# Attention inside a 1-core Trainium2 kernel: turned blocks of probabilities by 16 transfers a head between partitions, in place of five by way of memory

## The chip, the cores and the metric

One Trainium2 chip; the kernel uses one of its cores. A core has five engines that run side by side, each on its own instruction stream and in order: TensorE (PE, with the loading of its weights as PEld), VectorE (DVE), ScalarE (ACT), GpSimd (POOL) and SyncE (SP), which here does nothing but issue DMA transfers. The transfers themselves run on 16 DMA engines. Engines wait for one another and for transfers by semaphores.

The metric is the device time of one launch in microseconds (us), the median of the runs shown. Profiled executions are single executions with the hardware profiler on.

## The reference: what is computed

A transformer layer in float32, for 8 sequences of 512 tokens of width 256: attention with 16 query heads of width 128 in 4 groups (each group shares keys and values), then a feed-forward layer of 64 experts, six for a token, with a shared expert beside them. Each part has a normalization before and after it and a residual sum. Of the attention:

```python
q = q + pe
k = k + pe
scores = jnp.einsum('bgqtd,bgksd->bgqts', q, k) / math.sqrt(D)
causal = jnp.tril(jnp.ones((t, t), dtype=bool))
scores = jnp.where(causal, scores, -jnp.inf)
probs = jax.nn.softmax(scores, axis=-1)
out = jnp.einsum('bgqts,bgksd->btgqd', probs, v).reshape(b, t, G * QPG * D)
return out @ wo
```

The probabilities come out of the softmax with query tokens on the partitions. The product with `v` sums over key tokens, so it needs key tokens on the partitions: each 128 by 128 block of the probabilities has to be transposed. The change concerns how that is done.

## The kernel before

**Heads in a pipeline.** The outer loop (L884) runs over `k`, 0 to 127: 8 sequences of 16 heads. One iteration works on several heads at once, each at another step:

- `scores(k, i)` for the four tiles `i` of 128 query tokens (L887 and L888, then L893 and L894): TensorE multiplies queries and keys into `psc` (L280); DVE adds the causal mask, scales and finds the minimum into `e` (L284); ScalarE takes the exponential in place and sums rows (L287). Tile `i` has only its (i + 1) x 128 key columns, since the rest is masked.
- `turned(k - 1)` (L890), between the scores of tiles 1 and 2: the transposition, below.
- `weigh(k)` (L897): DVE takes reciprocals of the row sums (L294), GpSimd multiplies each `e` with them (L297).
- `project(k - 3)` (L900): the head's output times `wo`, summed over heads in PSUM (L352).
- `queries(k + 1)` (L907): the next head's queries, `pq` on TensorE (L267), bias and positions on DVE into `qt` (L270).
- `mix(k - 2)` (L909): probabilities times values into `pav` (L340), copied by ScalarE into `ao` (L108).

Between these, the loop calls the other work in small steps: the preparation of the next sequence (L929), the feed-forward part of the sequence before (`side`, L881), and, from head 94 on, the routed experts (`next(routed)`, L903 and others), 32 pairs of them, whose weights are loaded from memory by transfers that ScalarE issues (L515 and L522). After all pairs, the outputs of the first five sequences are finished with loads of `y_d` that SP issues (L650).

**Order.** The kernel is written with a schedule by hand: on each of the five engines, instructions run in the order in which the loop calls them. A DVE instruction that waits holds up every DVE instruction behind it, and a DMA that waits on SP holds up every DMA behind it on SP. Each transfer issued by SP or ScalarE counts up one of eight completion counters, given out in turn.

**Turning a head.** `e` holds 10 blocks of 128 by 128 on or under the diagonal. DVE's transpose turns squares of 32 by 32 in place, inside a group of 32 partitions. Six such instructions (L313) write the head into `eb`, laid out as (partition, `c`, block, `t`), where `c` says which group of 32 key tokens a square belongs to, and where the partition's group `a` says which group of 32 query tokens. A square is then right in itself, but stands in partition group `a`; for the product it has to be in group `c`. So squares must move from group to group, all 16 pairs (`c`, `a`), 32 partitions by 10 blocks x 32 values (1280 bytes) each. The kernel before does it through memory: SP stores `eb` whole into `ex_d` (L317, 640 KB; two such buffers), waits for it, and loads it back with four transfers (L320), one for each `c`, 32 partitions by four rows of 1280 bytes, into `et`. `mix` reads `et`.

`eb` has one buffer, `et` two, and each `e` two. The last two heads don't go this way: TensorE transposes them (`turned_at_once`, L323).

Of the kernel before, what the change touches and what calls it, by code (L numbers as in the profile page):

```python
# [22 lines left out]
NI = T // P  # L23
BS = 32
# [19 lines left out]
def sandwich_kernel(ctx, tc, x, wq, bq_t, wkv, bk_t, bv, wo, gate_wt, w_gate, w_up, w_down,  # L44
                    sh_gate_t, sh_up_t, sh_down_t, pe_t, out):
    nc = tc.nc
# [13 lines left out]
    ex_d = [dram.tile([P, NI, NB * BS], F32, tag=f"ex{n}_d", name=f"ex{n}_d") for n in range(2)]  # L60
# [61 lines left out]
    with ExitStack() as part:  # L122
# [180 lines left out]
        def turned(k):  # L303
            l = live[k]
            eb = p2.tile([P, NI, NB, BS], F32, tag="eb", name=f"eb_{k}", bufs=1)
            for i in range(NI):
                for js in ([0, 1], [2, 3]):
                    js = [j for j in js if j <= i]
                    if not js:
                        continue  # L310
                    at, step = AT[js[0]] + i - js[0], AT[js[-1]] - AT[js[0]] - 1
                    blocks = eb[:, :, at : at + step * (len(js) - 1) + 1 : max(step, 1), :]
                    nc.vector.transpose(  # L313
                        blocks.rearrange("p c j t -> p j c t"),
                        l["e"][i][:, js[0] * P : (js[-1] + 1) * P].rearrange("p (j c t) -> p j c t", c=NI, t=BS))
            ex = ex_d[k % 2]
            nc.sync.dma_start(out=ex, in_=eb.rearrange("p c n t -> p c (n t)"))  # L317
            l["et"] = p2.tile([P, NI, NB, BS], F32, tag="et", name=f"et_{k}")
            for c in range(NI):
                nc.sync.dma_start(out=l["et"][ts(c, BS)].rearrange("s a n t -> s a (n t)"),  # L320
                                  in_=ex[:, c, :].rearrange("(a s) f -> s a f", s=BS))

        def turned_at_once(k):  # L323

# [559 lines left out]
        for k in range(NK):  # L884
            b, s = divmod(k, NH)
# [3 lines left out]
            if 0 <= k - 1 < NK - 2:  # L889
                turned(k - 1)  # L890
# [136 lines left out]
```

## Time and profile before

| | us |
|---|---|
| median of 3 runs | 1485.7 |
| lowest and highest of them | 1483.86, 1485.82 |
| the profiled execution's own time | 1494.1 |
| its span, first to last instruction | 1492.3 |

Prediction and profile are compared by the profiled execution; it is 8.4 us above the median.

What the head loop's instructions take in it:

| Line | Engine | What | Count | Mean ns of one |
|---|---|---|---|---|
| L280 | PE | scores | 1024 | 445 |
| L340 | PE | probabilities times values | 1024 | 433 |
| L352 | PE | output projection | 1024 | 382 |
| L267 | PE | queries | 512 | 593 |
| L284 | DVE | mask, scale, minimum | 512 | 479 |
| L313 | DVE | transposes of 32 by 32 squares | 756 | 364 |
| L287 | ACT | exponential | 512 | 559 |
| L297 | POOL | weighing | 508 | 570 |

How to read the profile: the page has one line per engine (busy time, its share of the span, instructions), groups of instructions, and transfers by queue. The queue on which SP's transfers run moved 206.76 MB of 252.03 in all; memory was read for 143.01 MB and written for 107.74. In lists of waits, "A <- B: t, n, m" says that A waited t us in total for B, in n waits, the longest m us. In a timeline, "SPq" is SP's issuing of a transfer, not the transfer itself. Groups give the shortest, median and longest duration in ns.

### The profile page before, as it was taken

How to read it: one execution, taken by the hardware profiler on the slowest of the kernel's cores; microseconds unless marked ns; L12 is line 12 of the kernel's file. 1: busy time of each engine (PE TensorE's matmuls, PEld its weight loads, DVE VectorE, ACT ScalarE, POOL GpSimd, SP SyncE). 2: the span in 40 equal slices, each digit the busy share in tenths (PEclk: the TensorE clock that was granted, in tenths of full speed). 3: DMA queues.
4: the chain of work that ended last, by engine and by line, in shares of the span. 5: the costliest groups of instructions: out<-in, count | busy, mean ns of one | idle time of the engine just before them, and what ended most of it. 6: DMA issues, size and time to landing. Idle time of an engine off the chain costs nothing. (4 is left out here: it accounts for less than half of the span.)

```text
span 1492.3 us, 18593 instructions
## 1 busy us (share of the span) xinstructions
PE 1409.6 (94%) x5350; PEld 860.8 (58%) x5350; DVE 890.7 (60%) x3094; ACT 499.5 (33%) x1434; POOL 427.4 (29%) x682
## 2 busy tenths in 40 slices
PE   7999999999999999999999999988899998898894
PEld 3566655666656665666566666554555655565652
DVE  4565576657665676557665766665455454567442
ACT  1333343233332342233323332232333343344322
POOL 1222231124112322123112321144434344534202
PEclk9999999999999999999999999999999999999987
DMA  5764554355544464355435544469998899777511
GB/s 204 220 192 140 153 169 139 106 155 166 147 139 134 147 185 124 121 159 173 136 104 160 164 146 125 138 190 247 240 243 224 241 255 248 175 239 220 179 43 65
DMA packets 159702, 252.03 MB, mean 169 GB/s; under 512 B 16092, under 2 KB 135869, under 8 KB 159341
## 3 DMA queue, kind: packets, MB, share of 16 engines
q1 hardware_dynamic: 130061, 206.76, 46.5%
q10 hardware_dynamic: 23392, 34.61, 8.3%
q0 software_dynamic: 6144, 9.44, 3.4%
q8 instruction: 44, 0.72, 0.2%
q14 instruction: 61, 0.50, 0.1%
HBM read 143.01 MB, written 107.74 MB: 168 GB/s over the span
## 5 line engine op out<-in xcount | busy, mean ns | idle before, releaser
L297 POOL TENSOR_SCALAR e<-e,recip 128x128 f32<-128x128 f32 x508 | 269.6, 570 | 814.5 <-DVE recip L294 781.6
L287 ACT ACTIVATE e<-e,least 128x128 f32<-128x128 f32 (+3 forms) x512 | 285.8, 559 | 387.3 <-DVE least L284 356.0
L280 PE MATMUL psc<-kt,qt 128*128 128x128 f32 (+3 forms) x1024 | 312.7, 445 | 27.6 <-DVE least L284 8.7
L340 PE MATMUL pav<-et,v 128*128 128x512 f32 (+3 forms) x1024 | 297.2, 433 | 6.8 <-ACT dd L576 5.0
L340 PEld LDWEIGHTS pav<-et,v 128*128 128x128 f32 x1024 | 194.0, 190 | 170.1 <-issue 121.0
L284 DVE CUSTOM_DVE_ANT_0 e<-psc,mask 128x128 f32<-128x128 f32 (+3 forms) x512 | 231.7, 479 | 55.5 <-PE psc L280 49.6
L352 PE MATMUL po<-wo_sb,ao 128*128 128x256 f32 x1024 | 244.3, 382 | 0.7 <-ACT ao L108 0.7
L267 PE MATMUL pq<-xnt,wq_sb 128*128 128x512 f32 x512 | 240.8, 593 | 0.0
L352 PEld LDWEIGHTS po<-wo_sb,ao 128*128 128x128 f32 x1024 | 193.5, 191 | 69.3 <-issue 38.6
L280 PEld LDWEIGHTS psc<-kt,qt 128*128 128x128 f32 x1024 | 167.7, 193 | 108.7 <-DVE least L284 31.7
L313 DVE STREAM_TRANSPOSE eb<-e 128x128 f32<-128x128 f32 x756 | 227.4, 364 | 0.1
L108 ACT COPY ao<-pav 128x512 f32<-128x512 f32 x128 | 75.0, 586 | 445.3 <-PE pav L340 429.2
L270 DVE SCALAR_TENSOR_TENSOR qt<-pq,bq_sb,pe_sb 128x512 f32<-128x512 f32 x128 | 95.6, 747 | 115.0 <-PE pq L267 114.9
L267 PEld LDWEIGHTS pq<-xnt,wq_sb 128*128 128x128 f32 x512 | 95.9, 190 | 69.0 <-issue 63.5
L287 ACT ACTIVATION_READ_ACCUMULATOR e<-e,least 128x1 f32 x512 | 95.7, 187 | 0.0
L294 DVE RECIPROCAL recip<-total 128x4 f32<-128x4 f32 x128 | 22.8, 178 | 121.7 <-ACT e L287 121.7
L577 POOL DMA_INDIRECT y_d<-dd,idx x32 | 51.0, 1593 | 108.0 <-DMA y_d<-dd,idx 43.3
L239 PE MATMUL pk<-xnt,wkv_sb 128*128 128x512 f32 x128 | 61.3, 605 | 0.0
L252 DVE TENSOR_TENSOR v<-pv,bv_sb 128x512 f32<-128x512 f32 x32 | 22.1, 692 | 65.2 <-PE pv L250 65.2
L250 PE MATMUL pv<-wkv_sb,xnt 128*128 128x512 f32 x128 | 59.7, 593 | 0.0
L111 DVE COPY ht<-pth 88x256 f32<-88x256 f32 x32 | 13.4, 418 | 69.5 <-PE pth L558 69.4
L242 DVE SCALAR_TENSOR_TENSOR kt<-pk,bk_sb,pe_sb 128x512 f32<-128x512 f32 x32 | 24.0, 751 | 50.4 <-PE pk L239 50.4
(191 smaller groups left out, 1126.5 us busy)
## 6 DMA issues: line engine op xcount, KB each, us to landing
ex_d<-eb SPq DMA_DIRECT2D x126, 640.0 KB
et<-ex_d SPq DMA_DIRECT2D x504, 160.0 KB
wgu<-in_w_gate ACTq DMA_DIRECT2D x32, 352.0 KB
wgu<-in_w_up ACTq DMA_DIRECT2D x32, 352.0 KB
wd<-in_w_down ACTq DMA_DIRECT2D x32, 352.0 KB
y<-y_d SPq DMA_DIRECT2D x10, 512.0 KB
x<-in_x SPq DMA_DIRECT2D x8, 512.0 KB
x_d<-x SPq DMA_DIRECT2D x8, 512.0 KB
```

Of the source, the lines that this page charges most:

```text
L108: nc.scalar.copy(dst, src)
L239: nc.tensor.matmul(pk, lhsT=wkv_sb[:, c, g, 0, :], rhs=s["xnt"][:, c, :], start=c == 0, stop=c == NC - 1)
L250: nc.tensor.matmul(pv, lhsT=s["xnt"][:, c, ts(i, P)], rhs=wkv_sb[:, c, :, 1, :], start=c == 0, stop=c == NC - 1)
L267: nc.tensor.matmul(pq, lhsT=wq_sb[:, c, ts(h, D)], rhs=seqs[b]["xnt"][:, c, :], start=c == 0, stop=c == NC - 1)
L270: nc.vector.scalar_tensor_tensor(qt, pq, bq_sb[:, h : h + 1], pe_sb, ALU.add, ALU.add)
L280: nc.tensor.matmul(psc[:, :w], lhsT=l["qt"][:, ts(i, P)], rhs=seqs[b]["kt"][h // QPG][:, :w], start=True, stop=True)
L284: nc.vector.tensor_tensor_reduce(out=e, in0=psc[:, :w], in1=mask[:, T - w :], scale=-1.0 / math.sqrt(D), scalar=BIG, op0=ALU.add, op1=ALU. ...
L287: nc.scalar.activation(e, e, AF.Exp, bias=l["least"][:, i : i + 1], scale=-1.0, accum_out=l["total"][:, i : i + 1])
L297: engine.tensor_scalar(e, e, recip[:, n : n + 1], 1.0, ALU.mult, ALU.mult)
L313: nc.vector.transpose(blocks.rearrange("p c j t -> p j c t"), l["e"][i][:, js[0] * P : (js[-1] + 1) * P].rearrange("p (j c t) -> p j c t", ...
L340: nc.tensor.matmul(pav[:, :, j:, :], lhsT=seqs[b]["v"][:, j, ts(g, D)], rhs=l["et"][:, :, AT[j] : AT[j] + NI - j, :], start=j == 0, stop=j ...
L352: nc.tensor.matmul(po[b][i // 2][:, i % 2, :], lhsT=ao[:, ts(i, P)], rhs=wo_sb[:, h, :], start=h == 0 and i % 2 == 0, stop=h == NH - 1, sk ...
```

## The change

The store into `ex_d` and the four loads from it are gone. In their place SP issues 16 transfers for each head, one for every pair of groups, each from 32 partitions of `eb` straight into 32 partitions of `et`, 40 KB each. `ex_d` stays declared and unused. Nothing else is edited: the buffers, the six transposes and the readers of `et` are the same. In the built program the streams of PE, DVE, ACT and POOL hold the same instructions in the same order; only waits differ, since `eb` and `et` now each hang on 16 transfers.

```diff
@@ -313,12 +313,10 @@
                     nc.vector.transpose(
                         blocks.rearrange("p c j t -> p j c t"),
                         l["e"][i][:, js[0] * P : (js[-1] + 1) * P].rearrange("p (j c t) -> p j c t", c=NI, t=BS))
-            ex = ex_d[k % 2]
-            nc.sync.dma_start(out=ex, in_=eb.rearrange("p c n t -> p c (n t)"))
             l["et"] = p2.tile([P, NI, NB, BS], F32, tag="et", name=f"et_{k}")
             for c in range(NI):
-                nc.sync.dma_start(out=l["et"][ts(c, BS)].rearrange("s a n t -> s a (n t)"),
-                                  in_=ex[:, c, :].rearrange("(a s) f -> s a f", s=BS))
+                for a in range(NI):
+                    nc.sync.dma_start(out=l["et"][ts(c, BS), a], in_=eb[ts(a, BS), c])
 
         def turned_at_once(k):
 
```

## The prediction, made before the changed kernel ran

> **What bounds the kernel now.** The page comes first: who is busy.
>
> ```profile
> PE 1409.6 (94%) x5350; PEld 860.8 (58%) x5350; DVE 890.7 (60%) x3094; ACT 499.5 (33%) x1434; POOL 427.4 (29%) x682
> ```
>
> TensorE is busy 94% of the span. The table of busy time by stretch says where the other 6% lies; its columns are the stretch, its length, PE, PEld, DVE, ACT and POOL busy, the clock, the DMA share and GB/s.
>
> ```profile
> 37.00:174.00 137.00, 133.28 (x465) 82.10 (x465) 78.64 (x276) 48.66 (x144) 34.09 (x65) 1.00 0.60 177
> 496.00:657.00 161.00, 158.63 (x567) 98.24 (x566) 103.00 (x355) 54.07 (x161) 39.19 (x71) 1.00 0.48 145
> 980.00:1306.00 326.00, 302.38 (x1387) 175.53 (x1386) 175.98 (x631) 111.70 (x306) 142.89 (x166) 0.98 0.88 232
> ```
>
> A sequence of 16 heads (496 to 657) takes 161.0 us with 2.4 of TensorE idle: PE-bound, the path through memory hidden. In the expert stretch (980 to 1306) 23.6 us of TensorE are idle at a DMA share of 0.88. So no shorter path for the blocks can win much: up to 980 us there is almost nothing to win, after it at most some 25 us. The question is whether the new path stays hidden, so I read the queue that issues it, SP. Its waits:
>
> ```profile
> SPq L320 <- DMA ex_d<-eb: 443.0, 126, 9.3
> SPq L317 <- DVE eb L313: 436.2, 103, 9.8
> ```
>
> SP waits 443 us for the stores to memory (3.5 a head) and 436 us for the turned blocks: it has time to spare. Then its timeline over a sequence; columns are start, length, instruction, count. The reader is to see the distance from one store (L317) to the next.
>
> ```profile
> 495.86 0.34 SPq L317 DMA_DIRECT2D ex_d<-eb  x1
> 498.85 1.73 SPq L320 DMA_DIRECT2D et<-ex_d  x4
> 503.62 0.34 SPq L317 DMA_DIRECT2D ex_d<-eb  x1
> 511.38 0.34 SPq L317 DMA_DIRECT2D ex_d<-eb  x1
> ...
> 557.11 0.34 SPq L317 DMA_DIRECT2D ex_d<-eb  x1
> ...
> 570.24 0.34 SPq L317 DMA_DIRECT2D ex_d<-eb  x1
> ...
> 639.61 0.34 SPq L317 DMA_DIRECT2D ex_d<-eb  x1
> ...
> 649.09 0.34 SPq L317 DMA_DIRECT2D ex_d<-eb  x1
> ```
>
> A head takes 7.8 us where nothing else runs (503.62 to 511.38), 13.1 where a feed-forward step lies in it, 9.5 later on; the mean of 16 is 161/16 = 10.1. The whole timeline of one head shows what holds the one buffer `eb`:
>
> ```profile
> 705.48 1.81 DVE L313 STREAM_TRANSPOSE eb<-e 128x128 f32<-128x128 f32 x6
> ...
> 707.31 0.34 SPq L317 DMA_DIRECT2D ex_d<-eb  x1
> ...
> 711.11 1.73 SPq L320 DMA_DIRECT2D et<-ex_d  x4
> ```
>
> DVE turns for 1.81, SP issues 0.02 later, and `eb` is free when the store has landed: in quiet stretches 2.99 after its issue began (495.86 to 498.85). So `eb` is held 1.81 + 0.02 + 2.99 = 4.8 us, less than the shortest head: never seen as a wait.
>
> **What the Trainium skill says.** DMA: Bandwidth & Descriptors, Rules for kernel authors, wants many small transfers joined, "under 64 KB you're paying mostly overhead". The new ones have 40 KB. The trace agrees in kind: issuing a 160 KB load costs SP about as much as issuing a 640 KB store (rows below). Perfetto Trace Analysis, What "DMA-bound" means, names the issuing sequencer as a limit of its own, with only descriptor generation inside its slices; here the slice of 0.34 against a landing at 2.99 agrees. The price of SP's issue is what everything below hangs on.
>
> **The change, part by part.**
> 1. Removed: per head a 640 KB store, SP's wait for it, four 160 KB loads. That is 126 x 1.31 MB = 165 of the 252 MB moved. Below 980 us it frees nothing that bounds.
> 2. Added: 16 transfers of 40 KB, `et<-eb`, 32 partitions by 1280 bytes, 2,016 in all. No engine's order changes but SP's.
> 3. The price of one issue. No such transfer is in the trace. The nearest rows (shortest, median, longest ns), then the only small-partition store:
>
> ```profile
> L317 SPq DMA_DIRECT2D ex_d<-eb x126: 319/338/1781, 36.6 to 1393.2; - x126
> L320 SPq DMA_DIRECT2D et<-ex_d x504: 302/430/1542, 39.6 to 1397.6; - x168
> ```
>
> ```profile
> 35.32 0.52 SPq L200 DMA_DIRECT2D y_d<-zero  x1
> 35.88 0.58 SPq L204 DMA_DIRECT2D y_d<-zero  x1
> ```
>
> The four loads take 1.73 together: one each 0.475 in a row (0.43 and a gap of 0.045). That is the low end. The store of 64 partitions, fewer than 128 on both sides as the new ones have, took 0.52 with nothing in flight before it but one row, and its other copy, behind five transfers near 115 us, 1.07. In a row an issue is dearer than alone by 0.43 - 0.34 = 0.09, so 0.52 + 0.09 + 0.045 = 0.65 in a row. Against it: these have half the partitions. I take 0.60; high end 0.70. I set the 1.07 aside, since the other rows also have a long tail (1781, 1542) beside medians of 0.34 and 0.43.
> 4. The landing of the last one. The store's 2.99 holds the time for 640 KB; at the 435 GB/s that the same page gives in Where 436 GB/s comes from, 1.51. Left 1.48, and 0.09 for 40 KB: 1.57 from the issue's start, an estimate. A target in SBUF could answer sooner (to -0.4), contention make it later (+1).
> 5. The wait that takes the old one's place. `eb` has one buffer; DVE's first turn of the next head overwrites what all 16 transfers read, so it waits for the last. `eb` is now held 1.81 + 0.02 + 15 x 0.60 + 1.57 + 0.1 (DVE's waits on eight counters instead of one; at most 0.3) = **12.5 us**. DVE works in order: behind the turn stand the score evictions of tiles 2 and 3, the reciprocal and the next queries' bias; behind those ScalarE's exponentials, GpSimd's weighing and TensorE's next scores. No head can be shorter than 12.5. At 0.475 it is 10.6, at 0.70 14.0.
> 6. The other wait, TensorE's for `et` in `mix`, ends with the same transfers. `mix(k-1)` is called in the iteration after the one that turns head k-1, behind its scores, projection and queries; it isn't late before DVE is. The two or so wait instructions more a head on TensorE I cost at nothing: they stand before a `mix` that is queued behind 1.7 us of query matmuls.
> 7. In the built program each transfer waits on one of eight counters in turn, so for the one eight before it: 8 x 0.60 = 4.8 back, landed 3.2 ago. It costs nothing in quiet stretches. Where weights stream, ScalarE's loads share these counters: SP waits for weights, ScalarE for `et`.
>
> **The sum, against the profiled run's own 1494.1 (span 1492.3).** First 16 heads: 16 x 12.5 = 200 for 138: +62. (Each has two more issues, `y_d<-zero`, 0.9 us; SP then works 10.6 of 12.5.) The five sequences to 980 us: 806 natural, 80 x 12.5 = 1000: +194. I let the heads of 13 to 14.6 us be absorbed, since TensorE can run ahead of a waiting DVE by about 6 us (it stops where the next queries' bias is needed, 1.8 + 1.3 + 0.9 + 0.75 after the turn starts). If not, +3.5 a sequence. From 1302 to 1393: ten heads at 9 to 10 us become 12.5: +25, less 5 for what TensorE got ahead. Expert stretch: heads there last 13 to 25 us, so the loop seldom decides; less memory traffic could win back some of the 23.6 (say -10), the shared counters and 16 landings under load cost (0 to +60); I take +10. Together +286: 1780 profiled, and 8.4 less for the median (1485.7 against 1494.1): **1770 us**, 19% slower.
>
> **Rivals.**
> - Issue at the low end, 0.475: the loop is 10.6; first 16 heads +32, the five sequences 80 x 10.6 = 848 for 806, +42, the end +5: 1565. For it: the four loads are also 32 partitions wide on their SBUF side, and 32 rows should be no more work to issue than 128. Against: the 64-partition store.
> - Counters as the bound where weights stream: SP, ScalarE and TensorE wait for one another in turn. Some 19 heads at 16 us go to 20: +75 on top, 1845. For it: DMA share 0.88, SP already waits up to 9.3 us for a landing there. Against: two thirds of SP's own traffic is gone.
> - Faster: the freed memory traffic. If an issue costs under 0.40 in a row, the loop is under 9.5 us; PE-bound heads then hide it (at 9.5 it costs under 10 us), and the expert stretch gets back most of its 23.6 us, the `y<-y_d` loads (2% of the chain) some of their time: 1460. For it: issues that stood alone took 0.30 to 0.34. Against: no series in this trace is under 0.47, and these 16 are a series.
>
> **How the numbers follow.** Forecast case 0.72 (its own range 1640 to 1880, for issues of 0.53 to 0.68); low issue cost 0.11; counters 0.09; faster 0.05; the rest, 0.03, is a tie. Range 1580 to 1890: it takes in half of the first rival and of the second. A measurement can tell 0.2% from no change, 3 us: faster 0.05, within 0.03, slower 0.92.
>
> **What would show it.** In the profile after: the 2,016 issues with a median near 0.55, their starts 0.6 apart, first to first 12.5 us in nearly every head before 980; the largest wait of DVE's L313 one for `et<-eb`, with TensorE's share near 80%; HBM traffic down from 143 and 108 MB to about 60 and 25. Wrong if heads keep their 7.8 and 9.5 us (issue cheap), if starts are spread by waits on counters, or if TensorE's `mix`, not DVE's turn, is what waits.

## The result, and the profile after

The changed kernel takes 1919.31 us (1917.49 to 1919.78, 4 runs) against 1485.76 beside it: a ratio of 1.289, interval 1.286 to 1.291. The direction and the wait that takes over are as forecast. The size is not: 1770 was predicted with a range to 1890, and 1919 lies above it.

The profiled execution took 1917.5 us with a span of 1915.8. Its page first, the busy line, the chain that ended last by engine and by line, and the group of the turns, with the same group of the kernel before as the last line:

```profile
PE 1562.5 (82%) x5350; PEld 920.4 (48%) x5350; DVE 893.4 (47%) x3094; ACT 495.9 (26%) x1434; POOL 427.1 (22%) x682
...
HBM read 60.43 MB, written 25.17 MB: 45 GB/s over the span
...
SPq 44%; PE 20%; DMA 16%; DVE 11%; issue 6%; ACT 1%; DVEq 1%; POOL 0%; ACTq 0%; POOLq 0%
SPq L319 44%; DMA et<-eb 12%; DVE eb L313 9%; PE pav L338 4%; PE psc L280 3%; PE po L350 2%; PE pq L267 2%; PE py L682 2%; DMA x<-x_d 2%; PE pk L239 2%; DMA wd<-in_w_down 1%; PE psg L669 1%; PE pgu L539 1%; PE pv L250 1%; PE pd L565 1%
...
L313 DVE STREAM_TRANSPOSE eb<-e 128x128 f32<-128x128 f32 x756 | 228.0, 365 | 577.7 <-DMA et<-eb 533.8
...
L313 DVE STREAM_TRANSPOSE eb<-e 128x128 f32<-128x128 f32 x756 | 227.4, 364 | 0.1
```

Of the chain, 44% of the span is SP issuing L319, 12% the landing of its last transfer, 9% the turn: the loop on the one buffer `eb`. VectorE waits 534 us for it before its turns, where before it waited 0.1. (The chain of the kernel before can't be set beside this one: it reaches back only to 1284 us. That TensorE was the limit there is read from its busy share.) The change did what it says to memory, 85.6 MB read and written in place of 250.8.

The issues as a group (shortest, median, longest ns):

```profile
L319 SPq DMA_DIRECT2D et<-eb x2016: 507/589/1903, 36.9 to 1826.6; - x184
```

Then one head in the timeline of VectorE, two turns (start, length, instruction; in brackets the idle time before it and what ended it):

```profile
607.00 1.81 DVE L313 STREAM_TRANSPOSE eb<-e 128x128 f32<-128x128 f32 x6 [5.42 <-DMA et<-eb]
...
620.63 0.64 DVE L313 STREAM_TRANSPOSE eb<-e 128x128 f32<-128x128 f32 x2 [3.10 <-DMA et<-eb]
```

and between them, in the timeline of SP, the first and the sixteenth transfer of the head:

```profile
608.88 0.51 SPq L319 DMA_DIRECT2D et<-eb  x1
...
618.30 0.59 SPq L319 DMA_DIRECT2D et<-eb  x1
```

The turn ends at 608.81; SP starts 0.07 later; fifteen issues on, at 618.30, it starts the last; 2.33 after that VectorE may overwrite `eb`. From turn to turn 13.6 us. Over the first 96 heads the mean of this distance is 13.58, and it is nearly the same in every head (13.2 to 15.0), where before it went from 6.1 in the very first, 7.6 in those of the later sequences, to 14.6.

By stretch (columns as in the prediction), two sequences before 980 us in old terms, the second and the fourth:

```profile
251.00:470.00 219.00, 177.38 (x565) 105.15 (x566) 102.96 (x354) 54.06 (x161) 39.20 (x72) 0.93 0.22 59
690.00:905.00 215.00, 180.91 (x565) 106.70 (x565) 102.96 (x355) 54.08 (x161) 39.11 (x71) 0.91 0.22 60
```

161 us became 215 to 219. Note the DMA share of 0.22: bandwidth is not what is short. The time goes into SP's series of issues, with the turn before it and the landing after it.

### The profile page after: what moved, and what is told of

It reads as the page before. It is cut to its first block, busy times and chain, and to the rows that moved or that the text cites. A ratio compares the mean times of both kernels' runs of the same rounds, so it can differ in the third digit from the quotient of the medians.

```text
span 1915.8 us, 20423 instructions
## 1 busy us (share of the span) xinstructions
PE 1562.5 (82%) x5350; PEld 920.4 (48%) x5350; DVE 893.4 (47%) x3094; ACT 495.9 (26%) x1434; POOL 427.1 (22%) x682
## 4 chain that ended last, share of the span: by engine, by line
SPq 44%; PE 20%; DMA 16%; DVE 11%; issue 6%; ACT 1%; DVEq 1%; POOL 0%; ACTq 0%; POOLq 0%
SPq L319 44%; DMA et<-eb 12%; DVE eb L313 9%; PE pav L338 4%; PE psc L280 3%; PE po L350 2%; PE pq L267 2%; PE py L682 2%; DMA x<-x_d 2%; PE pk L239 2%; DMA wd<-in_w_down 1%; PE psg L669 1%; PE pgu L539 1%; PE pv L250 1%; PE pd L565 1%
## 5 line engine op out<-in xcount | busy, mean ns | idle before, releaser
L313 DVE STREAM_TRANSPOSE eb<-e 128x128 f32<-128x128 f32 x756 | 228.0, 365 | 577.7 <-DMA et<-eb 533.8
L338 PE MATMUL pav<-et,v 128*128 128x512 f32 (+3 forms) x1024 | 364.4, 507 | 139.5 <-DMA et<-eb 111.8
L280 PE MATMUL psc<-kt,qt 128*128 128x128 f32 (+3 forms) x1024 | 352.7, 487 | 113.7 <-DVE qt L270 96.9
L338 PEld LDWEIGHTS pav<-et,v 128*128 128x128 f32 x1024 | 217.7, 219 | 356.6 <-issue 258.7
L280 PEld LDWEIGHTS psc<-kt,qt 128*128 128x128 f32 x1024 | 182.6, 210 | 217.0 <-DVE qt L270 107.5
L350 PE MATMUL po<-wo_sb,ao 128*128 128x256 f32 x1024 | 258.9, 399 | 0.7 <-ACT ao L108 0.7
L267 PE MATMUL pq<-xnt,wq_sb 128*128 128x512 f32 x512 | 244.9, 601 | 0.0
L350 PEld LDWEIGHTS po<-wo_sb,ao 128*128 128x128 f32 x1024 | 205.2, 203 | 76.5 <-issue 40.3
L539 PE MATMUL pgu<-wgu,gxt 128*64 128x352 f32 x256 | 44.8, 471 | 5.1 <-DVE gxt L111 4.1
L682 PE MATMUL py<-sd_sb,hid 128*128 128x256 f32 (+1 forms) x192 | 45.8, 391 | 0.0
L118 PE MATMUL pt_f<-ident,xg 128*128 128x128 f32 x64 | 14.5, 365 | 36.3 <-DVE least L284 34.3
```

What stands on the lines that cost most here:

```text
L267: nc.tensor.matmul(pq, lhsT=wq_sb[:, c, ts(h, D)], rhs=seqs[b]["xnt"][:, c, :], start=c == 0, stop=c == NC - 1)
L280: nc.tensor.matmul(psc[:, :w], lhsT=l["qt"][:, ts(i, P)], rhs=seqs[b]["kt"][h // QPG][:, :w], start=True, stop=True)
L313: nc.vector.transpose(blocks.rearrange("p c j t -> p j c t"), l["e"][i][:, js[0] * P : (js[-1] + 1) * P].rearrange("p (j c t) -> p j c t", ...
L338: nc.tensor.matmul(pav[:, :, j:, :], lhsT=seqs[b]["v"][:, j, ts(g, D)], rhs=l["et"][:, :, AT[j] : AT[j] + NI - j, :], start=j == 0, stop=j ...
L350: nc.tensor.matmul(po[b][i // 2][:, i % 2, :], lhsT=ao[:, ts(i, P)], rhs=wo_sb[:, h, :], start=h == 0 and i % 2 == 0, stop=h == NH - 1, sk ...
L682: nc.tensor.matmul(py, lhsT=hid[:fw, n, ts(i, P)], rhs=sd_sb[:fw, n, :], start=first and n == 0, stop=last and n == len(SH_CHUNKS) - 1, sk ...
```

## The experiments

Four are about what the loop is made of, two about the price of one issue, four about a way out. Three kernels (one, eight, wide) fill `et` with the right number of bytes but not with the right squares. Their tokens are then routed otherwise and the kernel's last loop (L948) runs one pass more: TensorE counts 5452 instructions in place of 5350. That pass costs 59 to 63 us (in the run with one transfer 1519.9 - 1357 = 163 lie after the start of the last turn, 1492.3 - 1392 = 100 before). The totals of all three are read less 62; that the other routing changes nothing else is taken, not shown.

**One transfer in place of 16.**

```diff
-            for c in range(NI):
-                for a in range(NI):
-                    nc.sync.dma_start(out=l["et"][ts(c, BS), a], in_=eb[ts(a, BS), c])
+            nc.sync.dma_start(out=l["et"], in_=eb)
```

> One transfer of 640 KB from eb to et for a head in place of 16 (the squares are not moved to their groups, so the products are of other blocks; the same bytes arrive in the same buffer and the same waits are there). Theory A, the loop of issues on the single buffer eb: eb is held 1.81 (turn) + 0.06 + about 3.5 (one issue and the landing of 640 KB) = 5.4 us, less than the shortest head of 7.6, so up to 980 us the heads have their old lengths, and the total is 1486 or less; how much less is what the memory traffic was worth in the expert stretch, 10 to 25 us. Rival B, that a transfer between partitions itself is slow to land or collides with DVE and TensorE in SBUF: heads stay over 12 us, total over 1750.

1520.27 us, ratio 1.020 (1.017 to 1.023); less the extra pass some 1458, a gain somewhat above the 10 to 25 us expected. The heads have their old lengths up to 976 us (978 before). After that, in stretches that end with the start of the last turn, of this kernel:

```profile
976.00:1225.00 249.00, 243.67 (x1147) 142.17 (x1146) 143.27 (x507) 88.48 (x243) 113.11 (x130) 1.00 0.74 212
1225.00:1357.00 132.00, 128.13 (x557) 79.74 (x556) 95.81 (x336) 57.24 (x163) 63.08 (x84) 1.00 0.59 183
```

and of the kernel before, between the same heads:

```profile
978.00:1241.00 263.00, 247.79 (x1148) 144.28 (x1147) 143.02 (x508) 88.80 (x245) 112.26 (x129) 0.98 0.89 238
1241.00:1392.00 151.00, 133.81 (x558) 82.50 (x557) 94.64 (x340) 58.52 (x166) 62.54 (x85) 0.97 0.80 219
```

So a transfer with SBUF, the on-chip memory of `eb` and `et`, on both sides (here each row stays in its partition) is not slow in itself; with one issue in place of 16 it wins 14 + 19 = 33 us, all of it where the DMA share was high. That is about what the change could have brought. Whether the freed traffic or an earlier landing wins it is not told apart.

**Eight transfers of 80 KB.**

```diff
-                for a in range(NI):
-                    nc.sync.dma_start(out=l["et"][ts(c, BS), a], in_=eb[ts(a, BS), c])
+                for a in range(0, NI, 2):
+                    nc.sync.dma_start(out=l["et"][ts(c, BS), a : a + 2], in_=eb[ts((c + a) % NI, BS), a : a + 2])
```

> Eight transfers of 80 KB for a head, 32 partitions each, in place of 16 of 40 KB (two squares go together, to places that are not theirs; the same bytes fill the same buffer). Theory A: the loop is 1.81 + 0.06 + 7 x 0.633 + 2.25 = 8.6 us, shorter than most heads: total 1480 to 1500. Rival B, the bytes between partitions or their landing set the loop: unchanged, 1900.

1568.18 us, ratio 1.052 (1.049 to 1.055); less the pass about 1506, just above what was expected. Most of the shortest heads are now 8.5 to 8.7 us long from turn to turn, as worked out, and a sequence takes 167 us against 161. Each issue still has a median of 589 ns at twice the bytes: it is the count that costs.

**Twelve transfers, the squares that stay in their group copied by GpSimd:**

```diff
             for c in range(NI):
+                nc.gpsimd.tensor_copy(l["et"][ts(c, BS), c], eb[ts(c, BS), c])
                 for a in range(NI):
-                    nc.sync.dma_start(out=l["et"][ts(c, BS), a], in_=eb[ts(a, BS), c])
+                    if a != c:
+                        nc.sync.dma_start(out=l["et"][ts(c, BS), a], in_=eb[ts(a, BS), c])
```

> The change with one cut alone: the four squares that stay in their own group of partitions are copied by GpSimd, so SP issues 12 transfers and not 16; one buffer. Theory A: four issues fewer, 4 x 0.633 = 2.5 us less a loop: 13.5 becomes 11.0; 96 x 2.5 = 240 and about 30 at the end: 1650. If the loop hung on the last landing or the waits on eight counters and not on the count: 1850 or more.

1670.17 us, ratio 1.121 (1.117 to 1.125). Most heads that were shorter are now 10.8 to 11.2 long, and the total came 20 us above the 1650 expected. With 16, 12 and 8 transfers the loop is 13.5, 11.0 and 8.6: 0.61 for each transfer and 3.7 for the rest (the turn and the last landing). With these three counts on one line, the number of issues is shown as what sets the loop.

**A second `eb` for 88 heads.**

```diff
-            eb = p2.tile([P, NI, NB, BS], F32, tag="eb", name=f"eb_{k}", bufs=1)
+            eb = (p3.tile([P, NI, NB, BS], F32, tag="wgu", name=f"eb_{k}") if k < 88 else
+                  p2.tile([P, NI, NB, BS], F32, tag="eb", name=f"eb_{k}", bufs=1))
```

> The 16 transfers as in the change, but eb alternates between two buffers for the first 88 heads (it borrows the two buffers of the expert weights, which are unused until then); from head 88 on one buffer as before. Theory A: the turn and the last landing leave the loop, and SP's issuing alone sets the pace: 16 x 0.633 = 10.1, with the longer heads 10.3 in the mean against 13.55: 88 x 3.25 = 286 us less, total about 1635. If SP and not the buffer were all that counts, or the landing delays SP itself through the eight counters: nothing changes, 1919.

1731.95 us, ratio 1.162 (1.158 to 1.166): 187 us less than the change, not 286. VectorE's wait for `et<-eb` falls from 533.8 to 95.4, so the turn and the landing did leave the loop. But a sequence takes 182 to 186 us, not 10.3 x 16 = 165. The sum was too hopeful: long heads of 12.9 to 14.6 stay long, and only the short ones are lifted to 10.2; added head by head that gives 176. The other 7 or so lie around the sixth head of a sequence (15 us), where SP also stores and loads `x`, with a wait between (3.6 us in the one looked at, 449.7 to 453.3). SP's wait for the turn, in its list of waits:

```profile
SPq L320 <- DVE eb L314: 220.8, 58, 11.3
```

58 waits in 126 heads; the changed kernel had 115, of 416 us. In the other heads the next turn is done before SP is. So the second buffer is worth 187 us, and what is left in the short heads is SP's issuing.

**Sixteen transfers of 128 partitions**, to see what makes the issue dear:

```diff
-            for c in range(NI):
-                for a in range(NI):
-                    nc.sync.dma_start(out=l["et"][ts(c, BS), a], in_=eb[ts(a, BS), c])
+            for n in range(0, NI * NB * BS, 80):
+                nc.sync.dma_start(out=l["et"].rearrange("p a n t -> p (a n t)")[:, n : n + 80],
+                                  in_=eb.rearrange("p c n t -> p (c n t)")[:, n : n + 80])
```

> Sixteen transfers a head of all 128 partitions by 320 bytes, in place of 16 of 32 partitions by 1280 (squares not moved to their groups; the same bytes). Step 3 of the prediction put the dearer issue down to partitions fewer than 128 and left the four loads' 0.475 as the low end. If few partitions make it dear: issues 0.475 apart, loop 1.87 + 15 x 0.475 + 2.2 = 11.2 us, total about 1620. If any transfer from SBUF to SBUF is dear to issue: issues 0.63 apart, loop 13.5, total 1900 to 1930.

1906.16 us, ratio 1.279 (1.275 to 1.283), less the pass some 1844. Here `eb` is read in slices of 80 values, so the first issues start before the whole head is turned; a head takes 12.8 and not 13.5, which is why the corrected total lies under the 1900 expected. The price of an issue is what was asked. The group:

```profile
L318 SPq DMA_DIRECT2D et<-eb x2016: 464/599/1700, 36.7 to 1756.3; - x184
```

A median of 599 with all 128 partitions: it isn't the few partitions.

**Sixteen loads of the same shape, from memory.**

```diff
+            ex = ex_d[k % 2]
+            nc.sync.dma_start(out=ex, in_=eb.rearrange("p c n t -> p c (n t)"))
...
-                    nc.sync.dma_start(out=l["et"][ts(c, BS), a], in_=eb[ts(a, BS), c])
+                    nc.sync.dma_start(out=l["et"][ts(c, BS), a].rearrange("s n t -> s (n t)"), in_=ex[ts(a, BS), c, :])
```

> The way through memory, but with 16 loads of 40 KB (32 partitions by 1280 bytes) in place of four of 160: the same count and shape of transfers as in the change, with memory on the one side. If the dear issue (0.633 apart) belongs to a transfer that has SBUF on both sides: loads 0.475 apart, eb free when the store has landed as in the kernel before; SP then works 0.34 + 2.65 (waiting for the store) + 16 x 0.475 = 10.6 a head, which sets the pace of the shorter heads (the sum of the longer of 10.8 and each head's old length is some 13 us a sequence more, 60 in the first): 1590 to 1640. If it is the count or the 40 KB that make an issue dear: 0.63 apart, 13.1 a head, over 1850.

1738.34 us, ratio 1.166 (1.161 to 1.171): outside both expectations. Its issues and two of its heads:

```profile
L321 SPq DMA_DIRECT2D et<-ex_d x2016: 302/419/1972, 40.4 to 1649.8; - x184
```

```profile
658.45 7.28 SPq L321 DMA_DIRECT2D et<-ex_d  x16
665.83 0.37 SPq L317 DMA_DIRECT2D ex_d<-eb  x1
668.88 7.48 SPq L321 DMA_DIRECT2D et<-ex_d  x16
676.46 0.56 SPq L317 DMA_DIRECT2D ex_d<-eb  x1
```

The price is told apart: 419 ns and 0.46 from one to the next for 32 partitions by 1280 bytes from memory, 589 and 0.63 between partitions. The total was missed by the sum. Redone with the old lengths, the longer of 10.8 and each head's own comes to 22 us a sequence more, not 13, and measured were 24 to 29. After head 96 some 65 us came on top (288 and 190 us, where before took 263 and 150), for which the expectation had nothing. So 16 small transfers cost some 250 us even with memory on one side and `eb` free once the store has landed.

**Half the issues off SP.** Four squares by GpSimd, four issued by ScalarE after `weigh(k)`, eight by SP, two buffers for 88 heads:

```diff
...
+            l["rest"] = []
             for c in range(NI):
+                nc.gpsimd.tensor_copy(l["et"][ts(c, BS), c], eb[ts(c, BS), c])
                 for a in range(NI):
-                    nc.sync.dma_start(out=l["et"][ts(c, BS), a], in_=eb[ts(a, BS), c])
+                    if a == (c + 1) % NI:
+                        l["rest"].append((l["et"][ts(c, BS), a], eb[ts(a, BS), c]))
+                    elif a != c:
+                        nc.sync.dma_start(out=l["et"][ts(c, BS), a], in_=eb[ts(a, BS), c])
...
             weigh(k)
+            for dst, src in live.get(k - 1, {}).pop("rest", ()):
+                nc.scalar.dma_start(out=dst, in_=src)
```

> The change with SP's share of the issuing cut to half: the four squares that stay in their group are copied by GpSimd, four of the other twelve are issued by ScalarE after its exponentials, eight by SP; eb alternates between two buffers in the first 88 heads. Theory A (issues in series on SP are the bound): SP needs 8 x 0.633 = 5.1 us a head, the loop with one buffer would be 1.87 + 7 x 0.633 + 2.2 = 8.5; up to 980 us the heads have their old lengths, and the expert stretch and the end win what the single transfer won there, some 30 us: 1450 to 1475. Rival: ScalarE and GpSimd, now waiting for the turned blocks in order, pass the wait on (ScalarE's copies of the outputs, GpSimd's weighing): 1500 to 1600.

**The same from head 96 on only**, with one buffer, the first 96 heads by way of memory (the edit is the same, behind a test of `k < 96`):

> The way through memory for the first 96 heads, word for word as before, and from head 96 on the direct one with its issues shared as in the run with half the issues on SP, one buffer. Theory A: the first 96 heads are bound by TensorE either way, so it wins what is to be won after 980 us, about 30 us against before: 1450 to 1465. Rival, that ScalarE's four issues a head stand in the way of its weight loads there: no gain, 1485 to 1500.

1518.68 us, ratio 1.019 (1.016 to 1.022), and 1514.77, ratio 1.016 (1.013 to 1.019), outside both of its expectations. Up to head 96 theory A holds (984 us and 980, for 978). In the expert stretch the rival holds, and by more than was expected of the second: 291 and 294 us where before took 263. The last heads win some 6 us back (144 and 145, for 150). The waits of the first of the two in that stretch:

```profile
POOL et L320 <- DMA y_d<-dd,idx: 42.0, 12, 5.9
...
ACT dd L580 <- DMA et<-eb: 23.1, 5, 7.3
```

GpSimd's copies queue behind its own scatters of expert outputs, and ScalarE, which issues weight loads on the shared counters, waits for `et`. With GpSimd's copies but no issues of ScalarE's (the twelve transfers above) the stretch took 269.6, so ScalarE's part looks the larger; that was not isolated.

**Half direct, half by memory, from head 96 on**, everything issued by SP and the direct ones while the store lands. The edit is against the kernel before (the second kernel has 3 for the 2):

```diff
-            nc.sync.dma_start(out=ex, in_=eb.rearrange("p c n t -> p c (n t)"))
+            m = NI if k < 96 else 2
+            nc.sync.dma_start(out=ex[:, :m, :], in_=eb[:, :m].rearrange("p c n t -> p c (n t)"))
...
-            for c in range(NI):
+            for c in range(m, NI):
+                for a in range(NI):
+                    nc.sync.dma_start(out=l["et"][ts(c, BS), a], in_=eb[ts(a, BS), c])
+            for c in range(m):
```

> The way through memory as before for 96 heads. From head 96 on, half of each: SP stores two of the four groups (320 KB), issues the eight direct transfers of the other two while that store lands, then the two loads. The result is the reference's. Theory A: SP's series is 0.34 + 8 x 0.633 + 2 x 0.475 and never waits for the store, the loop is 1.87 + 0.34 + 7 x 0.633 + 0.6 + 1.0 + 2.2 = 10 us at most, seldom longer than a head there (9 to 24), and half of the blocks' memory traffic is gone: the expert stretch takes some 253 us and the last heads some 137, as in the run with eight transfers, against 263 and 150: 1460 to 1470. Rival: eight more waits on the shared completion counters cost what the traffic saves: 1485 to 1500.

> The same with one group direct (four transfers) and three by way of memory from head 96 on. Theory A: a quarter of the traffic saved and four issues: about half of the other's gain, 1472 to 1482. Rival, counters: 1485 to 1495.

Half: 1490.31 us, ratio 1.000 (0.999 to 1.001), no gain, where its rival put it. A quarter: 1472.03, ratio 0.987 (0.984 to 0.990), at the low end of what was expected; 1.3% less than before, and the interval is clear of 1. Its two stretches, between the same heads as above:

```profile
983.00:1239.00 256.00, 244.91 (x1149) 143.42 (x1148) 143.97 (x510) 89.16 (x246) 113.41 (x130) 1.00 0.87 235
1239.00:1376.00 137.00, 128.93 (x557) 79.79 (x556) 95.06 (x335) 57.12 (x163) 62.18 (x84) 1.00 0.78 221
```

7 and 14 us less than before, at only 9.8 MB less traffic (30 heads of 160 KB less stored and loaded). The half took 258.9 and 148.6 in its profile, which is 6.5 us under its own median. It takes twice as much traffic away and gains less, so the freed traffic alone doesn't explain the quarter's gain; why the half gives back in the last heads what the quarter keeps there was not found.

## Why the prediction was wrong

The mechanism was right: VectorE's turn waits for the last of 16 issues in series. What failed is the size of two terms of the loop's sum, the price of an issue (step 3: 9.43 us in place of 9.0 for fifteen) and the landing of the last one (step 4: 2.21 in place of 1.67 with VectorE's waits). They made a loop of 13.5 out of the 12.5 of step 5, and the range did not take in the ends that the text itself set. By the prediction's steps:

- Steps 1 and 2 hold. The freed traffic bought nothing before 980 us (shown by the single transfer), and only SP's stream changed.
- Step 3, the price of an issue, failed by a little in size and altogether in reason. Taken was 0.60; measured 0.633 from start to start. The 64-partition store had pointed to 0.65; the discount for "half the partitions" is refuted, since 128 partitions cost as much (599 ns). What separates the prices of the blocks' transfers in these runs is whether memory stands on one side. By that the store, which goes to memory, should have been cheap; why it was dear stays open, and that it came near was luck.
- Step 4, the landing, failed most: 1.57, with 0.1 for VectorE's waits, was taken for the time from the last issue's start to VectorE's next turn; it is 2.21 (median over the first 95 heads; 2.33 in the head shown). It was scaled from a store whose issue takes 0.34, while the issue here takes 0.59, and the step counted from the issue's start: that is 0.25 of the 0.54. The rest was not split between landing and the waits on eight counters.
- Step 5 holds as a mechanism: VectorE's L313 waits 534 us for `et<-eb`, and one head is as long as the next. Its sum was 12.5, measured 13.5 (1.81 + 0.06 + 9.43 + 2.21). Over 96 heads, 13.58 - 12.5 = 1.08 makes 104 us of the 137 that were missing (1917.5 against 1780).
- The long heads were absorbed, as the sum assumed. (Its run-ahead of about 6 us is not what its four figures add up to, 4.75; nothing hung on it.) At shorter loops they are not: with eight transfers, a loop of 8.6, the short heads grew and the long ones stayed, 6 us in every sequence. So the faster case's "under 10 us" for a loop of 9.5 was too little.
- Step 6 half holds. `mix` does wait for `et` (112 us, 48 times), but second to VectorE: all lengths follow VectorE's loop.
- Step 7 holds in quiet stretches: SP waited for earlier `et<-eb` transfers 9.7 us in all. In the expert stretch the +10 was too small. A wait there that goes by the counters:

```profile
ACT ao L108 <- DMA et<-eb: 21.7, 4, 9.6
```

ScalarE's copy of `ao` stands behind weight loads that wait for `et`. The stretch took 286 us for 263, +23, where +10 was taken, and the last heads 190 for 150, +39, where +20 was taken. Together 33 us, the rest of the gap. With 13.5 or its old length for each head, whichever is longer, +11 and +35 come out: the loop makes most of the second and about half of the first, where the prediction let it decide seldom.
- Of the rivals, the low issue price fell with the median of 589 ns, the faster case with it. The counters' wait exists, at some 20 us on ScalarE and not 75; what it cost in total was not isolated.
- The range ended at 1890. With the high end of the issue, 0.70, the loop was put at 14.0, and a landing one us later at 13.5 with the price taken; 96 heads at 14.0 in place of 12.5 are 144 us more, 1914. The bounds had been worked out and the range was drawn inside them.

## What to carry to other kernels

Before splitting a transfer, multiply the count by the issuing engine's time for one, add what fills the buffer and what it takes until its last reader is done, and compare with the shortest iteration: a buffer without a twin turns that sum into the length of the loop. The path off memory won here only in stretches where the DMA share was 0.8 to 0.9 (33 us with a single transfer), and nothing where it was about 0.5; a quarter of the blocks moved over there, and none elsewhere, beat both kernels. And where two neighbours give two prices, the range has to reach what the dearer one makes of the whole sum.

## What the runs showed of the hardware that was not expected

- A transfer with SBUF on both sides takes SP 589 to 599 ns to issue in a series, 32 or 128 partitions, 320, 1280 or 2560 bytes each; from memory into SBUF 419 to 430. Alone, 465 (the single transfer) against 338 for the store of the same 640 KB to memory; the first of the 16 with nothing just ahead of it takes 507. On ScalarE 542 (median in the run with half the issues off SP; 601 in the one from head 96 on).
- An issue's time also depends on the issue ahead of it. The same store of `x` to memory, before (L729, behind loads from memory) and after (L727, behind an `et<-eb` issue), shortest, median and longest in ns:

```profile
L729 SPq DMA_DIRECT2D x_d<-x x7: 382/382/382, 212.0 to 1307.3; - x7
L727 SPq DMA_DIRECT2D x_d<-x x7: 523/528/529, 318.9 to 1700.1; - x7
```

With 16 loads from memory ahead of it, it has a median of 382 again. So a price is best read from start to start in a series, and not from one issue.
- TensorE took longer for the same instructions. Its busy time rose by 153 us, and the 1024 products of L338 took 507 ns each in the mean, in place of 433 (L340 before). In the trace the granted clock is either whole or half. It stood at half in 71 stretches, 334 us in all, where before it was 7 stretches and 55 us; the 0.88 to 0.93 by sequence are means of the two. Products of L338 that touch such a stretch took 765 ns in the mean, the others 431, as before. In the run with one transfer, without gaps in the heads, the clock stood whole until after the last turn, and the products (there L336) took 433 again. That the gaps bring the half clock fits these runs; it was not tested by itself. A busy time that grows here goes with the stall and is not its cause.
